# Counting samples by plain comparisons, summed on TensorE and ScalarE, and centring x right behind X W0, in a four-layer graph kernel

## The chip, the cores and the metric

The kernel runs on one core of a Trainium2 chip. A core has five engines that run side by side, each with a queue of its own that it works through in order: TensorE (PE, with its weight loads as PEld), VectorE (DVE), ScalarE (ACT), GpSimd (POOL) and SyncE (SP), which here only issues transfers. They wait for each other by semaphores. The metric is the device time of one execution in microseconds; the median over several runs counts.

## The reference

The input is `x` (2708 x 128), a weighted adjacency `adj` (2708 x 2708, non-negative and sparse, but stored dense), and the weights of four layers. Each layer is `x = layernorm(x + layer(x, adj))`. The two layers that matter here are 0 and 1:

```python
# layer 0
A_hat = A + eye;  degree = A_hat.sum(axis=1);  d = degree ** -0.5
h = (d[:, None] * A_hat * d[None, :]) @ X
return h @ W.T + b
# layer 1
XW = X @ W
Z1 = leaky_relu(s_row[:, None] + s_col[None, :], 0.01)   # s_row, s_col: XW times two vectors
den = exp(Z1);  num = A @ den
att = where(num != 0, den / num, 0)
return A @ (att @ XW)
```

Layer 2 is a hyperbolic graph convolution, layer 3 a sum over signed neighbours; both multiply by the whole adjacency once or more. They lie behind the change and are not touched by it.

## The kernel before

Features are kept as rows: `x` lies in memory as 128 feature partitions by 2708 nodes. Nodes are cut into 22 tiles of 128 (`NT`) and into 6 column blocks of up to 512 (`NB`). The kernel passes through four stages.

*Stage 1, loads and degrees.* L837 computes z = X W0 per node tile (`node_major_products`), evicted by ScalarE. Then for each column block c the adjacency tiles A(d, c), d = 0..5, are loaded by SyncE (`load_tile`, one MB each), VectorE adds them into `part` (L1084, L1086), `degrees(c, part)` (L870) folds `part` further and multiplies it by ones on TensorE (`deg`, L880), ScalarE takes the root (L891), and VectorE scales rows of z. `multiply` (L855, the products at L860) adds z times A into one PSUM accumulator per block. After blocks 0 and 1, `centred` (L921) subtracts the feature mean from three blocks of x each: a TensorE product with `centre_w`, copied back into x by ScalarE. ScalarE also checks every tile for negative entries (L1060).

*Stage 2, the end of layer 0 and the head of layer 1.* A loop over c = 0..4 (L1111) has three parts per turn. Each part issues a third of the last products of block c (`last_products`). In between, for block c-1, come `norm_roots` (variance on TensorE, root on ScalarE, reciprocal and split into three terms on VectorE), `normed` (spreading by TensorE, `rs`, and multiplication into x by VectorE), `projected` (x times W1 and the two attention vectors on TensorE, `xw`, copied out by ScalarE into `rc` and `xw`), `clamped`, and for block c-2 or c-1 `count`. Blocks 4 and 5 are finished behind the loop (L1129 to L1143).

*Counting.* The nodes are to be sorted by their attention scores into 26 groups (`GM`) of at most 126. For this, 384 scores are taken as `samples` (the scores of tiles 1 to 3), and for each of the 22 tiles and each of two scores the kernel asks of every sample how many nodes lie above it, and of every node how many samples it lies below. `count` does both in a single VectorE instruction per tile and score, 44 in all (L1041): `counts = (samples > node) + counts`, with the row sum going to `counted`.

*Stage 3, sorting.* L1176 to L1181 sum `counts` over the partitions on TensorE (`below`), VectorE derives limits (`lim`, `jp`, `prev`) and follows the group borders in a chain of 26 steps (`jk`, L1228); then come each node's group, slot and the lists. Meanwhile TensorE computes `whole_sum` (L790, products at L797), a product of exponentials `e1` with the whole adjacency, four steps at first (L1161) and the others spread over the sorting. `e1` comes from ScalarE (L1159).

*Stage 4* is the grouped attention and layers 2 and 3, from 240 us to the end.

The order in stages 2 and 3 is written by hand: under `with queued(E)` every instruction on engine E is issued behind the last one that was queued on E. So for TensorE, ScalarE and VectorE the order of the queue is the order of the calls in the program. Outside of `queued`, a scheduler orders the instructions.

PSUM has eight banks: `acc0` to `acc5` and a pair `ps` which is used in turn.

Of the kernel before, what the change touches and what calls it, by code (L numbers as in the profile page):

```python
# [21 lines left out]
P = 128  # L22
# [35 lines left out]
def kernel(  # L58
# [655 lines left out]
    counts = col.tile([P, 2, NS], BF16, tag="counts", name="counts")  # L714
    nc.gpsimd.memset(counts, 0.0)
    counted = col.tile([P, 2, NT + 1], F32, tag="counted", name="counted")
    nc.gpsimd.memset(counted[:, :, 0:1], 0.0)
# [72 lines left out]
    def whole_sum(n):  # L790
        if not tot:
            tot.extend(acc_tile(i, f"t1_{i}") for i in range(2))
# [42 lines left out]
    with tc.tile_pool(name="tri", bufs=1) as tp:  # L835
        z = q_b.rearrange("p (t f) -> p t f", f=F)
        node_major_products(w0T_s, F, lambda t0, m, ps: nc.scalar.copy(z[:, t0 : t0 + m, :], ps))  # L837
        dcol = c_tile("dcol")
# [31 lines left out]
        def degrees(c, part):  # L870
# [7 lines left out]
            for i, t in enumerate(ts):  # L878
                kw = rows(t)
                nc.tensor.matmul(  # L880
                    pd[:kw, i : i + 1], lhsT=part[:, 0, i * P : i * P + kw], rhs=ones[:, 0:1], start=True, stop=True
                )
# [37 lines left out]

        def centred(blocks):  # L921

            for b in blocks:
                w, cs = width(b), bslice(b)
                xc = ps_tile(f"xc{b}")
                nc.tensor.matmul(xc[:, :w], lhsT=centre_w, rhs=x[:, cs], start=True, stop=True)
                nc.scalar.copy(x[:, cs], xc[:, :w])
# [107 lines left out]

        def count(c, a=0, b=8):


            with queued(DVE):
                for t, i in itertools.islice(itertools.product(tiles(c), range(2)), a, b):  # L1040
                    nc.vector.scalar_tensor_tensor(  # L1041
                        counts[:, i, :],
                        samples,
                        cmp_v[:, i, t : t + 1],
                        counts[:, i, :],
                        op0=ALU.is_gt,
                        op1=ALU.add,
                        accum_out=counted[:, i, t + 1 : t + 2],
                    )

# [18 lines left out]
        for c in range(NB):  # L1069
# [3 lines left out]
            for d in range(NB):  # L1073
# [11 lines left out]
                elif d > 1:  # L1085
                    nc.vector.tensor_add(part[:, :nt, :w], part[:, :nt, :w], at[d][:, :nt, :w])  # L1086
# [4 lines left out]
            scaled, rooted[:] = degrees(c, part)  # L1091
            for d in range(NB - 2, NB):
                check(d, c, at[d])
            if c < 2:
                centred(range(3 * c, 3 * c + 3))
# [15 lines left out]
        for c in range(NB - 1):  # L1111
            for part in range(3):
                last_products(c, part)
                if c and part == 0:
                    norm_roots(c - 1)
                    if c > 1:
                        count(c - 2, 4, 7)
                elif c and part == 1:
                    normed(c - 1)
                    if c > 1:  # L1120
                        count(c - 2, 7)
# [9 lines left out]
        count(NB - 3, 1, 3)  # L1131
        norm_roots(NB - 2)
        norm_roots(NB - 1)
        count(NB - 3, 3, 6)
        normed(NB - 2)
        normed(NB - 1)
        count(NB - 3, 6)
        projected(NB - 2)
        projected(NB - 1)
        clamped(NB - 2)  # L1140
        count(NB - 2)
        clamped(NB - 1)
        count(NB - 1)  # L1143

# [4 lines left out]
    with ctx_keep:  # L1149
# [16 lines left out]
        with tc.tile_pool(name="sort", bufs=1) as st_p:  # L1166
# [7 lines left out]
            below_s = [acc_tile(4 + i, f"below{i}") for i in range(2)]  # L1174
            with queued(PE):
                nc.tensor.matmul(below_s[0][:, :NS], lhsT=ones_b, rhs=counts[:, 0, :], start=True, stop=True)  # L1176
            for i in range(2):
                if i:
                    nc.tensor.matmul(below_s[i][:, :NS], lhsT=ones_b, rhs=counts[:, i, :], start=True, stop=True)
# [728 lines left out]
```

## Time and profile before

| | us |
|---|---|
| median of 3 runs | 934.11 (933.47 to 936.2) |
| the profiled execution | 931.1 |
| its span | 929.4 |
| PE busy in the span | 856.4 (92%) |
| DVE busy | 564.3 (61%) |
| ACT busy | 369.6 (40%) |
| POOL busy | 152.5 (16%) |

A profile line of a group of instructions names the line of the kernel, the engine, the operation, what it writes and reads, the shapes and the count. In a timeline the first two numbers are start and length in us; a bracket behind gives the idle time before the instruction and what ended it. In the chain of waits, the program is followed back from its last instruction to whatever released each step. A row of stretches gives for each engine its busy time and number of instructions in that stretch, then the granted TensorE clock (1.00 is full), the share in which the DMA engines were busy, and GB/s.

The stages stand in the trace as follows: stage 1 from 0 to about 118 us, stage 2 to about 182 us, stage 3 to about 240 us, stage 4 to 929.4 us. The 44 counts run from 135.5 to 182.0 us.

### The profile page before, as it was taken

What the parts mean: (1) busy time and instruction counts of PE and PEld (TensorE: products, weight loads), DVE (VectorE), ACT (ScalarE), POOL (GpSimd) and SP (SyncE); (2) the same over time, 40 slices, a digit from 0 to 9 for tenths busy, and PEclk for the clock granted to TensorE, in tenths of its full rate; (3) what the DMA queues carried; (4) which work ended last, traced back from release to release, by engine and by line L of the source; (5) the groups of instructions that cost most, each with busy time, mean ns of one, the idle gap of its engine ahead of it and who ended that gap; (6) DMA issues with size and microseconds to landing.
All of it is one profiled execution on the core that took longest, in us unless ns stands there. A gap on an engine that the chain in (4) does not pass through costs nothing.

```text
span 929.4 us, 9409 instructions
## 1 busy us (share of the span) xinstructions
PE 856.4 (92%) x3268; PEld 428.0 (46%) x3268; DVE 564.3 (61%) x1221; ACT 369.6 (40%) x601; POOL 152.5 (16%) x182
## 2 busy tenths in 40 slices
PE   3799988579799999999999999989999999999997
PEld 2344534235344444444444444454344455555555
DVE  4895569898488888878786222637554464333222
ACT  3885332110677777566664111536332221000000
POOL 5321000303655554222110000000000000000000
PEclk9799999798799999999999999999999999999999
DMA  9997492195596555344431876477956293746410
GB/s 338 373 351 240 52 310 67 43 386 217 172 356 204 163 154 162 121 131 138 150 120 44 290 268 240 152 253 258 334 186 226 63 343 115 250 144 242 142 55 15
DMA packets 95834, 182.84 MB, mean 197 GB/s; under 512 B 6430, under 2 KB 23535, under 8 KB 95652
## 3 DMA queue, kind: packets, MB, share of 16 engines
q1 hardware_dynamic: 85556, 142.37, 44.5%
q0 software_dynamic: 8352, 37.76, 12.9%
q10 hardware_dynamic: 1872, 2.04, 0.6%
q8 instruction: 27, 0.44, 0.2%
q14 instruction: 27, 0.22, 0.1%
HBM read 179.33 MB, written 2.84 MB: 196 GB/s over the span
## 4 chain that ended last, share of the span: by engine, by line
PE 77%; DVE 14%; DMA 5%; ACT 2%; issue 2%; ACTq 0%; DVEq 0%
PE a L1518 21%; PE uacc L1426 14%; PE a L1797 11%; PE a L860 9%; PE num L1461 7%; PE a L1806 6%; DVE att L1474 4%; DMA A<-in_adjT_dram 4%; PE t L797 2%; DVE jk L1228 2%; DVE att L1455 2%; DMA cb<-in_adjT_dram 1%; PE pp L1755 1%; DVE counts L1041 1%; PE low L1293 1%
## 5 line engine op out<-in xcount | busy, mean ns | idle before, releaser
L1426 PE MATMUL uacc<-att,xw_g 128*128 128x512 f32 (+1 forms) x312 | 130.4, 554 | 8.9 <-DVE att L1474 8.2
L1466 ACT ACTIVATE ln<-num,inval,occ_l 128x512 f32<-128x512 f32 (+1 forms) x156 | 106.5, 722 | 65.7 <-DVE gat L1465 63.3
L1797 PE MATMUL a<-cb,ut 128*128 128x512 f32 (+2 forms) x264 | 124.8, 554 | 0.4 <-DMA cb<-in_adjT_dram 0.4
L1806 PE MATMUL a<-mask,node 128*128 128x512 f32 (+2 forms) x264 | 119.5, 534 | 0.0
L1461 PE MATMUL num<-gat,w_all 128*128 128x512 f32 (+1 forms) x276 | 114.1, 543 | 0.0
L1518 PE MATMUL a<-cb,q_b 128*128 128x512 f32 (+2 forms) x264 | 110.3, 555 | 1.7 <-DMA cb<-in_adjT_dram 1.7
L1518 PE MATMUL a<-cb,xw 128*128 128x512 f32 (+2 forms) x264 | 107.4, 550 | 0.0
L860 PE MATMUL a<-A,q_b 128*128 128x512 f32 (+2 forms) x264 | 105.8, 549 | 0.0
L1417 POOL DMA_INDIRECT gat<-in_adjT_dram,row_i x52 | 78.4, 1508 | 146.4 <-PE num L1461 79.4
L1426 PEld LDWEIGHTS uacc<-att,xw_g 128*128 128x128 f32 x312 | 55.8, 189 | 90.7 <-issue 50.0
L1465 DVE COPY gat<-num 2x512 f32<-2x512 f32 x150 | 86.0, 608 | 3.3 <-PE num L1461 3.1
L1474 DVE TENSOR_TENSOR att<-att,ln 128x1354 f32<-128x1354 f32 x52 | 81.1, 1560 | 9.6 <-ACT ln L1473 9.6
L1455 DVE TENSOR_SCALAR att<-q_b,gj_l 128x1354 f32<-128x1354 f32 x52 | 47.8, 921 | 37.8 <-PE uacc L1426 37.8
L1806 PEld LDWEIGHTS a<-mask,node 128*128 128x128 f32 (+1 forms) x264 | 47.7, 190 | 49.3 <-issue 47.5
L1461 PEld LDWEIGHTS num<-gat,w_all 128*128 128x128 f32 x276 | 51.2, 191 | 41.4 <-issue 22.7
L1473 ACT ACTIVATE ln<-ln 128x1354 f32<-128x1354 f32 x52 | 69.3, 1333 | 1.3
L1785 DVE TENSOR_SCALAR mask<-cb 128x3072 fp32r<-128x3072 f32 (+5 forms) x24 | 33.5, 1394 | 58.8 <-PE a L1806 58.6
L860 PEld LDWEIGHTS a<-A,q_b 128*128 128x128 f32 (+1 forms) x264 | 45.6, 190 | 47.9 <-issue 46.9
L1518 PEld LDWEIGHTS a<-cb,xw 128*128 128x128 f32 (+1 forms) x264 | 45.0, 190 | 46.3 <-issue 46.3
L1518 PEld LDWEIGHTS a<-cb,q_b 128*128 128x128 f32 (+1 forms) x264 | 44.6, 189 | 46.2 <-issue 42.3
L231 ACT ACTIVATE sq_l<-s 128x512 f32<-128x512 f32 (+1 forms) x11 | 6.6, 604 | 147.1 <-DVE s L1815 116.7
L1060 ACT ACTIVATE xw<-A 128x2048 f32<-128x2048 f32 (+3 forms) x36 | 57.0, 1583 | 8.2 <-issue 4.4
(446 smaller groups left out, 904.7 us busy)
## 6 DMA issues: line engine op xcount, KB each, us to landing
cb<-in_adjT_dram SPq DMA_DIRECT2D x15, 2816.0 KB
cb<-in_adjT_dram SPq DMA_DIRECT2D x15, 2560.0 KB
A<-in_adjT_dram SPq DMA_DIRECT2D x25, 1024.0 KB
B<-in_adjT_dram SPq DMA_DIRECT2D x18, 1024.0 KB
cb<-in_adjT_dram SPq DMA_DIRECT2D x3, 814.0 KB
cb<-in_adjT_dram SPq DMA_DIRECT2D x3, 740.0 KB
ut<-in_adjT_dram SPq DMA_DIRECT2D x2, 1024.0 KB
A<-in_adjT_dram SPq DMA_DIRECT2D x5, 296.0 KB
```

Of the source, the lines that this page charges most:

```text
L860: nc.tensor.matmul(acc[c][:, :w], lhsT=z[:kw, k, :], rhs=t[:kw, i, :w], start=c not in begun, stop=(d == NB - 1 and k == NT - 1), skip_gro ...
L1417: return nc.gpsimd.indirect_dma_start(out=gat[g], out_offset=None, in_=adj_h, in_offset=bass.IndirectOffsetOnAxis(ap=row_i[:, h, g : g + 1 ...
L1426: nc.tensor.matmul(uacc[c][:, : cb - ca], lhsT=xw_g[:, g, :], rhs=att[:, ca:cb], start=(g == 0), stop=(g == GM - 1),)
L1455: nc.vector.tensor_scalar(att, q_b[:, h0 : h0 + HALF], gj_l[:, g : g + 1], 1.0, op0=ALU.mult, op1=ALU.max)
L1461: nc.tensor.matmul(num[:, : cb - ca], lhsT=(w_first if g < FIRST else w_all)[:, g, :], rhs=gat[g][:, ca:cb], start=True, stop=True)
L1465: nc.vector.tensor_copy(gat[g + 1][0:2, ca:cb], num[0:2, : cb - ca])
L1466: nc.scalar.activation(ln_n[:, ca:cb], num[:, : cb - ca], AF.Ln, scale=occ_l[:, g : g + 1], bias=inval[:, g : g + 1],)
L1473: nc.scalar.activation(ln_n, ln_n, AF.Exp, scale=-1.0)
L1474: nc.vector.tensor_mul(att, att, ln_n)
L1518: nc.tensor.matmul(acc[:, :w], lhsT=weights[:kw, k, :], rhs=pc[:kw, t, :w], start=(k == 0), stop=(k == NT - 1),)
L1797: nc.tensor.matmul(acc[:, :w], lhsT=edge[:ke, k, :], rhs=pc[:ke, t, :w], start=(k == 0), stop=False, skip_group_check=True,)
L1806: nc.tensor.matmul(acc[:, :w], lhsT=node[:kw, k, j, :], rhs=mask[:kw, t - ma, :w], start=False, stop=(k == NT - 1 and j == 1), skip_group_ ...
```

## The change

It has four parts.

1. `count` becomes a plain comparison: `above = samples > node`, bf16, in a buffer of its own (five in rotation). A new `count_up` sums what is pending: TensorE multiplies `above` by ones into one of four groups of 32 rows of a PSUM tile (`acc0`), by the parity of the tile and the score, and ScalarE reads `above` with a Relu whose accumulator gives the row sum for `counted`. It is called in every part of the loop and between the last steps behind it.
2. The sum over partitions behind it reads the four row groups, copied once out of PSUM, with selecting weights `kind`; `lim` is one instruction; the test for the group uses the count itself with the opposite sign, so `upto` goes.
3. `centred` goes; all six blocks are centred right behind X W0.
4. In column block 0 the last tile A(5, 0) is not added by VectorE; `degrees` adds its two filled row tiles on TensorE.

PSUM banks of `whole_sum` and of the slots (`low`) move by one, since `acc0` is taken longer.

```diff
-    counts = col.tile([P, 2, NS], BF16, tag="counts", name="counts")
-    nc.gpsimd.memset(counts, 0.0)
-    counted = col.tile([P, 2, NT + 1], F32, tag="counted", name="counted")
+    counted = col.tile([P, 2, NT], F32, tag="counted", name="counted")
+    kind = const.tile([P, 2], F32, tag="kind", name="kind")
...
         node_major_products(w0T_s, F, lambda t0, m, ps: nc.scalar.copy(z[:, t0 : t0 + m, :], ps))
+
+        for b in range(NB):
+            w, cs = width(b), bslice(b)
+            xc = ps_tile(f"xc{b}")
+            nc.tensor.matmul(xc[:, :w], lhsT=centre_w, rhs=x[:, cs], start=True, stop=True)
+            nc.scalar.copy(x[:, cs], xc[:, :w])
...
+                terms = [] if more is None else [more[:, q, :] for q in range(2)]
+                terms.append(part[:, 0, :])
+                for q, a in enumerate(terms):
+                    nc.tensor.matmul(
+                        pd[:kw, i : i + 1],
+                        lhsT=a[:, i * P : i * P + kw],
+                        rhs=ones[:, 0:1],
+                        start=(q == 0),
+                        stop=(q == len(terms) - 1),
+                    )
...
         def count(c, a=0, b=8):
-            with queued(DVE):
-                for t, i in itertools.islice(itertools.product(tiles(c), range(2)), a, b):
-                    nc.vector.scalar_tensor_tensor(
-                        counts[:, i, :], samples, cmp_v[:, i, t : t + 1], counts[:, i, :],
-                        op0=ALU.is_gt, op1=ALU.add, accum_out=counted[:, i, t + 1 : t + 2])
+            for t, i in itertools.islice(itertools.product(tiles(c), range(2)), a, b):
+                above = tp.tile([P, NS], BF16, tag="above", name=f"above{t}_{i}", bufs=5)
+                with queued(DVE):
+                    nc.vector.tensor_scalar(above, samples, cmp_v[:, i, t : t + 1], None, op0=ALU.is_gt)
+                pending.append((t, i, above))
+
+        def count_up():
...
+            for t, i, above in pending:
+                j = 2 * (t % 2) + i
+                with queued(PE):
+                    nc.tensor.matmul(
+                        counts_of["below"][32 * j : 32 * j + 32, :NS],
+                        lhsT=ones_b[:, :32],
+                        rhs=above,
+                        start=(t < 2),
+                        stop=(t >= NT - 2),
+                        skip_group_check=True,
+                    )
+                with queued(ACT):
+                    nc.scalar.activation(counts_of["junk"], above, AF.Relu, accum_out=counted[:, i, t : t + 1])
+            pending.clear()
...
-                elif d > 1:
+                elif d > 1 and (d, c) != (NB - 1, 0):
...
-            scaled, rooted[:] = degrees(c, part)
+            scaled, rooted[:] = degrees(c, part, at[NB - 1] if c == 0 else None)
...
-            if c < 2:
-                centred(range(3 * c, 3 * c + 3))
...
-                if c and part == 0:
-                    norm_roots(c - 1)
-                    if c > 1:
-                        count(c - 2, 4, 7)
-                elif c and part == 1:
-                    normed(c - 1)
-                    if c > 1:
-                        count(c - 2, 7)
+                if c and part < 2:
+                    (normed if part else norm_roots)(c - 1)
+                if pending:
+                    count_up()
+                if c > 1 and part < 2:
+                    count(c - 2, *((7, 8) if part else (4, 7)))
...
         summed_up(NB - 1)
-        count(NB - 3, 1, 3)
         norm_roots(NB - 2)
+        count_up()
         norm_roots(NB - 1)
-        count(NB - 3, 3, 6)
+        count(NB - 3, 1, 4)
         normed(NB - 2)
+        count(NB - 3, 4, 6)
+        count_up()
         normed(NB - 1)
+        projected(NB - 2)
         count(NB - 3, 6)
-        projected(NB - 2)
+        count_up()
         projected(NB - 1)
         clamped(NB - 2)
-        count(NB - 2)
+        count(NB - 2, 0, 4)
+        count_up()
         clamped(NB - 1)
+        count(NB - 2, 4)
+        count_up()
         count(NB - 1)
+        count_up()
...
+            counts = srt([P, NS], "counts", F32R)
+            nc.vector.tensor_copy(counts, counts_of["below"][:, :NS])
```

## The prediction

> **What bounds the kernel now.** I read the page, then the busy time by stretches, then the chain of waits over the stretch that the change edits, then single instructions there. Only 0 to 190 us are edited; from 190 us on, sorting, attention and products are the same instructions and start from one result, the `below` matmuls of L1176. So the question is when `below` is done (184.3 us), and whether what follows moves with it. It does: behind it come the VectorE chain `jp`, `prev`, `jk` and the slots, without a wait that an outside event sets.
>
> Busy time by stretches (length, then PE, PEld, DVE, ACT, POOL, clock, DMA):
>
> ```profile
> 140.00:149.00 9.00, 8.00 (x40) 3.75 (x41) 8.79 (x28) 2.35 (x7) 0.00 (x0) 1.00 0.37 118
> 149.00:159.00 10.00, 9.14 (x49) 4.81 (x47) 9.12 (x30) 2.36 (x7) 0.19 (x1) 1.00 0.09 26
> 159.00:168.00 9.00, 5.65 (x38) 3.21 (x36) 8.57 (x26) 2.64 (x9) 0.00 (x0) 0.95 0.10 32
> ```
>
> VectorE looks like the bound (8.79 of 9.00), but TensorE is as full in the first two rows: two engines are near their limit, and relief of one meets the other. ScalarE has room.
>
> The chain of waits in order of time (start, length, what):
>
> ```profile
> 172.00 2.98 PE xw L993 x12
> 175.01 0.16 ACT rc L1002
> 175.17 0.28 ACT xw L1003
> 175.47 1.28 ACT L1159
> 176.76 0.21 ACT e L1159
> 176.97 0.04 issue
> 177.02 6.72 PE t L797 x58
> 183.74 0.27 PE below L1176
> ```
>
> This matters most. ScalarE's exponential (L1159, with its table load) releases TensorE's `whole_sum(4)` (6.72 us), and `below` is queued behind that. The last 12 counts run on VectorE at 174.76 to 182.05 beside it, and end 1.6 us before TensorE is free: they are hidden.
>
> Single instructions (start, length, engine):
>
> ```profile
> 145.97 0.37 ACT L972 ACTIVATE work<-var,eps_c 128x128 f32<-128x128 f32 x1 [0.94 <-PE var L252]
> 146.51 0.95 DVE L974 RECIPROCAL work<-work 128x128 f32<-128x128 f32 x1
> 148.81 0.40 PE L273 MATMUL rs<-work,sel 128*128 128x128 bf16 x4 [1.00 <-DVE work L267]
> 155.74 0.37 ACT L972 ACTIVATE work<-var,eps_c 128x128 f32<-128x128 f32 x1 [1.83 <-PE var L252]
> 156.14 0.95 DVE L974 RECIPROCAL work<-work 128x128 f32<-128x128 f32 x1 [0.67 <-ACT work L972]
> 158.44 0.40 PE L273 MATMUL rs<-work,sel 128*128 128x128 bf16 x4 [0.86 <-DVE work L267]
> 118.58 0.44 ACT L1060 ACTIVATE xw<-A 128x296 f32<-128x296 f32 x1
> 118.93 0.18 ACT L1060 ACTIVATION_READ_ACCUMULATOR xw<-A 128x1 f32 x1
> ```
>
> In the first loop counting delays the reciprocal by 0.14 us after the root; in the second VectorE itself waits 0.67 us. TensorE waits 1.00 and 0.86 us for `rs` in these loops: that is all VectorE can give them.
>
> **What the Trainium skill says.** "VectorE: DVE Perf Modes", section Mode 2×_2P: a single-source fp32 operation with both ends in SBUF does two elements per cycle. The trace agrees: `att` of L1455, 1354 elements, takes 0.92 us, below one per cycle (1.41). "ScalarE: Activation LUTs", section What ACT_TABLE_LOAD costs: an ACTIVATE with immediates takes 186 ns + 0.833 ns an element, overlapping by about 93 ns; the 296-element row above (0.44, accumulator read after 0.35) fits. Same page, Table sets: relu is in every set, so no load is added; L1060 and L891 run here after one load. "TensorE: Matmul & The Clock Gate", Part 3: matmuls of 32 output columns run beside each other; the eight `var` matmuls (0.43 us together) agree.
>
> **The change part by part.**
>
> *Comparisons.* Before, 44 fused compare-and-add run 0.54 us apart. Now they are plain comparisons: 384/1.92 = 0.20 us plus a fixed 0.14 (0.54 less 384/0.96; `ohs`, 128 elements, runs 0.163 apart): 0.34. Bounds: 0.26 if only synchronization remains, 0.54 if the double rate fails. VectorE sheds 44 x 0.20 = 8.8 us.
>
> *Sums on TensorE.* 44 matmuls of 384 bf16 columns. L1176 and L1179 give 0.17 us each alone; in column groups four may cost as little as 0.2 together. They stand in TensorE's queue. The four after `norm_roots` fit into the wait for `rs`. The next three stand between `rs` and the last products, and wait for three comparisons that VectorE starts only after the split into terms: 3 x 0.34 + 0.06 + 0.17 - 0.05 = 1.20 us after the start of `rs` instead of 0.23, so 0.97 lost; one more before `xw` costs 0.17. So 1.14 for each of the loops c = 2, 3, 4. Against that the reciprocal comes 0.25 earlier in c = 2, about 0.1 in c = 3, and 0.48 in the first count (139.94 to 139.46). Sum: 3 x 1.14 - 0.83 = +2.6. Bounds: -1.7 (the three TensorE waits shrink and the matmuls cost little) to +4.5.
>
> *After the loop.* Two comparisons fewer before the reciprocals and three cheaper ones give some 1.5 us; `rs` of block 5 now stands behind five sums, and `rc` of block 5 behind seven ScalarE sums: the same again and a little more. I take +0.3.
>
> *Sums on ScalarE.* Each is 384 elements: 0.35 + 88 x 0.00078 = 0.42, and 0.10 to the next after the accumulator read: 0.52 back to back, 0.64 if the accumulator read is waited for (the rows of 104.86 us stand 0.82 apart at 592 elements). In the loops ScalarE is 26% busy and takes them, behind each root in its queue. But the last 12 belong to blocks 4 and 5, follow the last `xw` copy, and the exponential of L1159 is issued behind them. So table load, exponential, `whole_sum(4)` and `below` all move by 12 x 0.55 = 6.6 us (6.2 to 7.7). What hid the counts, `whole_sum(4)`, is now behind them.
>
> *Centring.* Six blocks of two matmuls leave 29.4 to 34.9 and 45.2 to 48.6 us and go behind X W0, where TensorE stands idle for 9.28 us before 27.71; ScalarE's six copies (3.3 us) fall into its idle 4.42 us there. Up to 61 us the loads fill the DMA queues (DMA share 1.05, 375 GB/s) and VectorE's partial sums keep pace with 0.2 to 0.4 us to spare, so the first stretch gives nothing. Of the second, 1.82 + 0.52 = 2.3 us are in TensorE's chain, which is unbroken to 117 us. But the degree matmul of 60.46 waits for VectorE until 60.22 anyway; the gain exists only as far as products with A(0,3), which lands at about 59, are put ahead of it. Bounds 0 to 2.3; I take 1.3.
>
> *Degrees of column 0.* One addition of 1.3 us leaves VectorE and eight matmuls come (some 1.0 to 1.8 us by the two `deg` rows, 1.02 and 1.84 for eight instructions). Under the DMA bound: 0, with +1 if it overruns the 0.2 us to spare.
>
> *The rest.* The copy of `counts` (about 0.56 as `samples` L1032) lies beside `whole_sum`; `upto` (0.20) and a `lim` (0.16) leave; bank numbers change: 0. DMA reloads of `B` start later by the same shift as their readers, so nothing more.
>
> Sum: 2.6 + 0.3 + 6.6 - 1.3 = +8.2 us. The profiled execution took 931.1 us (span 929.4 and 1.7 around it): 939.3. It lies 3.0 below the median of 934.11, so on the median I forecast 942.3, rounded 942.
>
> **The rivals.**
> 1. *The loops are VectorE's alone.* For it: 8.79 of 9.00. Against: TensorE's waits there sum to about 3 us, and VectorE waited 0.67. If 32 comparisons before `rc` of block 5 save 0.28 each, `rc` comes 9.0 earlier; -9.0 + 6.6 - 1.3 = -3.7: 930.4, faster. It decides from 8.1 us won before the last `xw` copy.
> 2. *Centring wins nothing*, since column 2's degrees are set by loads (or the scheduler puts the matmuls elsewhere): +9.5, 943.6.
> 3. *The dear ends*: comparisons at one per cycle (3 loops x 3 x 0.2 = 1.8), ScalarE sums at 0.64 (1.1): +11.1, 945.2.
> 4. *The cheap ends*: -1.7 in the loops, 6.2 in the tail, -2.3 for centring, nothing after the loop: +2.2, 936.3, inside what measurement tells from no change.
>
> **How the numbers follow.** About 0.3% (2.8 us) is what can be told from no change. Chances: my forecast 0.45, rival 2 0.22, rival 3 0.13, rival 4 0.10, rival 1 0.10. Slower 0.80, same 0.10, faster 0.10. The forecast's own range is 938 to 945; with half of rival 4 and rival 3 it becomes 937 to 946.
>
> **What would show it.** Right: ScalarE runs 12 Relu with accumulators between the last `xw` copy and the exponential, over 6 us; `whole_sum` starts that much later against `rc` of block 5; distances between `rs` of 9.7 to 10.8 instead of 8.87 and 9.63; no `xc` after 27 us. Wrong: `rc` of block 5 before 170 us, an exponential ahead of the sums, or ScalarE sums shorter than 0.4 us. A first stage longer than before would show that the early `xc` delays the degrees of column 0.

## The result, and the profile after

The change makes the kernel slower: 947.71 us median (946.71 to 949.74, 4 runs) against 933.79 (933.06 to 936.2, 4 runs), a ratio of 1.0147 with a 95% interval of 1.0122 to 1.0172. The same kernel, run again later beside others, gave 950.63 (947.12 to 950.97, 5 runs), ratio 1.0183 (1.0161 to 1.0204). The forecast was 942, from 937 to 946.

Both kernels were profiled twice in the end, so that a difference can be told from the spread of one kernel. In us from the start of the span; `rs` is the first spread of a block, distances run from start to start, and the last two rows lie behind the change:

| | before, two profiles | after, two profiles | forecast of the change | measured |
|---|---|---|---|---|
| degree sums of block 1 start | 44.34, 45.26 | 46.05, 46.15 | | |
| first `rs` (end of stage 1) | 130.09, 131.10 | 131.23, 131.33 | -1.3 | +0.7 |
| first `rs` to that of block 4 | 37.59, 38.79 | 41.93, 40.69 | +2.6 | +3.1 |
| that to the last copy of `xw` | 7.39, 7.40 | 8.77, 8.78 | +0.3 | +1.4 |
| that to `below` | 8.60, 6.73 | 16.09, 16.29 | +6.6 | +8.5 |
| `below` to the first `num` | 60.10, 60.00 | 60.06, 59.75 | 0 | -0.1 |
| `num` to the end of the span | 685.6, 685.6 | 687.6, 688.6 | 0 | +2.5 |

"Measured" is the difference of the two means. From the second row on the rows sum to 16.1, which is the difference between the profiled times (947.42 and 947.12 against 931.1 and 931.35). A mean of two is worth about a microsecond here: the columns show how far one kernel differs from itself.

First what the engines do in the loops. Busy time by stretches of the kernel after, in the columns of before (length, then PE, PEld, DVE, ACT, POOL, clock, DMA):

```profile
140.00:149.00 9.00, 8.56 (x40) 3.69 (x42) 6.90 (x19) 6.41 (x22) 0.00 (x0) 1.00 0.19 57
149.00:159.00 10.00, 9.30 (x51) 4.74 (x44) 7.26 (x19) 7.17 (x23) 0.34 (x1) 1.00 0.10 27
159.00:168.00 9.00, 8.30 (x42) 3.44 (x40) 5.52 (x13) 5.87 (x21) 0.00 (x0) 1.00 0.01 3
```

VectorE has fallen from 8.79 to 6.90 us in the first row: it was relieved as intended. ScalarE has risen from 2.35 to 6.41. TensorE, full before, is full still, and the loops are longer. What one comparison and its two sums cost, for all 44 (shortest, median and longest in ns, then first and last start):

```profile
L1053 DVE TENSOR_SCALAR above<-samples,cmp_v x44: 401/414/2366, 137.8 to 187.7; 128x384 bf16<-128x384 f32 x44
L1065 PE MATMUL counts<-above,ones_b x44: 322/326/502, 139.0 to 188.2; 128*32 128x384 bf16 x44
L1074 ACT ACTIVATE above_j<-above x44: 511/523/536, 139.5 to 189.3; 128x384 bf16<-128x384 bf16 x44
L1074 ACT ACTIVATION_READ_ACCUMULATOR above_j<-above x44: 185/186/203, 139.9 to 189.8; 128x1 f32 x44
```

The comparison is cheap: 0.41 us long, three of them in 1.07 us, 0.33 apart where the forecast took 0.34. One of the 44 is not; it lasts until a GpSimd instruction beside it has ended:

```profile
184.27 2.67 POOL L1177 MEMSET xw<- 2x2816 f32 x1 [30.29 <-DMA xw_d<-xw]
184.80 2.37 DVE L1053 TENSOR_SCALAR above<-samples,cmp_v 128x384 bf16<-128x384 f32 x1 [0.23 <-ACT above_j L1074]
```

The sum on ScalarE is not cheap either: 0.52 us and 0.19 for reading out its accumulator.

One turn of the loop, single instructions of the kernel after in order of start (start, length, engine, line):

```profile
160.65 0.95 DVE L983 RECIPROCAL work<-work 128x128 f32<-128x128 f32 x1 [1.82 <-ACT work L981]
...
162.81 1.07 DVE L1053 TENSOR_SCALAR above<-samples,cmp_v 128x384 bf16<-128x384 f32 x3
...
162.95 0.40 PE L273 MATMUL rs<-work,sel 128*128 128x128 bf16 x4 [0.69 <-DVE work L267]
...
163.28 0.98 PE L1065 MATMUL counts<-above,ones_b 128*32 128x384 bf16 x3
...
164.19 2.18 PE L870 MATMUL a<-A,q_b 128*128 128x512 f32 x4
```

VectorE now waits 1.82 us for the root, where it had counted before. TensorE still waits 0.69 us ahead of `rs`, and then its last products stand behind three sums: they start 1.24 us after `rs`, where they started 0.23 after it.

The chain of waits at the end of the stretch:

```profile
189.32 0.61 ACT above_j L1074 x2
189.96 1.28 ACT L1189
191.25 0.21 ACT e L1189
...
191.51 6.58 PE t L801 x58
198.09 0.37 PE below L1210
```

The same exponential and the same `whole_sum` as in the first profile of before, 14.5 us later. What is ahead of them on ScalarE, right behind the last copy of `xw` (181.93 to 182.30):

```profile
182.20 0.53 ACT L1074 ACTIVATE above_j<-above 128x384 bf16<-128x384 bf16 x1
182.62 0.20 ACT L1074 ACTIVATION_READ_ACCUMULATOR above_j<-above 128x1 f32 x1
182.85 0.52 ACT L1074 ACTIVATE above_j<-above 128x384 bf16<-128x384 bf16 x1
...
189.96 1.28 ACT L1189 ACT_TABLE_LOAD   x1
```

Twelve sums, 0.645 us apart, from 182.20 to 189.94: 7.7 us, and the table load starts when the last one is done.

### The profile page after: what moved, and what is told of

Its sections match the earlier page's. It is cut to its first block, busy times and chain, and to the rows that moved or that the text cites. A ratio compares the mean times of both kernels' runs of the same rounds, so it can differ in the third digit from the quotient of the medians.

```text
span 945.7 us, 9626 instructions
## 1 busy us (share of the span) xinstructions
PE 874.5 (92%) x3328; PEld 435.8 (46%) x3328; DVE 557.5 (59%) x1175; ACT 396.2 (42%) x689; POOL 151.2 (16%) x186
## 4 chain that ended last, share of the span: by engine, by line
PE 75%; DVE 15%; DMA 2%; issue 2%; ACT 2%; ACTq 0%; DVEq 0%
PE a L1554 21%; PE uacc L1462 13%; PE a L1833 11%; PE a L870 9%; PE num L1497 7%; PE a L1842 6%; DVE att L1510 5%; DMA cb<-in_adjT_dram 2%; DVE att L1491 2%; DVE jk L1266 2%; PE t L801 1%; PE pp L1791 1%; DVE ut L1112 1%; PE xw L1002 1%; DVE work L983 1%
## 5 line engine op out<-in xcount | busy, mean ns | idle before, releaser
L870 PE MATMUL a<-A,q_b 128*128 128x512 f32 (+2 forms) x264 | 110.3, 568 | 2.3 <-DVE q_b L912 2.2
```

What stands on the lines that cost most here:

```text
L870: nc.tensor.matmul(acc[c][:, :w], lhsT=z[:kw, k, :], rhs=t[:kw, i, :w], start=c not in begun, stop=(d == NB - 1 and k == NT - 1), skip_gro ...
```

## The experiments

All times are medians; a ratio is to runs of the kernel before on the same chip.

| run | time | ratio, 95% interval |
|---|---|---|
| exp_first | 940.22 | 1.0059 (1.0042 to 1.0075) |
| later_three | 944.72 | 1.0119 (1.0100 to 1.0138) |
| comb (both) | 938.15 | 1.0042 (1.0024 to 1.0061) |
| comb2 | 935.94 | 1.0020 (1.0009 to 1.0031) |
| comb3 | 936.16 | 1.0019 (1.0006 to 1.0033) |
| loop_end | 947.31 | 1.0159 (1.0131 to 1.0188) |
| xc_back | 952.68 | 1.0182 (1.0156 to 1.0208) |
| more_back | 948.98 | 1.0158 (1.0140 to 1.0177) |
| both_back | 951.02 | 1.0171 (1.0143 to 1.0200) |
| filler | 947.11 | 1.0131 (1.0104 to 1.0158) |
| after_again | 950.63 | 1.0183 (1.0161 to 1.0204) |
| both_again | 948.60 | 1.0170 (1.0145 to 1.0195) |
| before_xc | 933.84 | 0.9990 (0.9971 to 1.0009) |
| before_early | 932.27 | 0.9986 (0.9976 to 0.9996) |
| before_two | 931.32 | 0.9972 (0.9959 to 0.9985) |

The medians are of 4 or 5 runs, of 12 to 22 for comb, comb2, comb3 and the last three. A sixteenth run, before_again, is the kernel before for its second profile (931.35, one execution).

Differences between two rows are often no larger than their intervals: those of after (1.0122 to 1.0172) and later_three overlap, those of exp_first and comb, of comb and comb2, of comb2 and comb3 too. Where that is so, the distances in the profiles carry the argument.

### The tail: the exponential ahead of the last twelve sums

In exp_first the exponential and `whole_sum(4)` go ahead of the sums of blocks 4 and 5; the twelve comparisons get room in `q_b`, so that none waits for a buffer.

```diff
         projected(NB - 1)
+        with queued(ACT):
+            nc.scalar.activation(e1[:, : tiles(1)[0]], rcl[:, 0, : tiles(1)[0]], AF.Exp)
+        with queued(PE):
+            whole_sum(4)
         clamped(NB - 2)
```

> The changed kernel with the exponential of the first four columns and the first four steps of the whole sum issued right behind the last projection, ahead of the last 12 comparisons' sums; the 12 comparisons get places of their own in a tile that is free by then, so that VectorE does not wait for ScalarE. Theory (the 12 row sums on ScalarE, 0.645 us each, stand between the last projection and the exponential, and the whole sum waits for it): the exponential starts about 1.5 us behind the last copy instead of 9, the below products end about 5 us earlier (near 193 instead of 198.9 us), time near 942.5 us. Rival (the counts themselves, by VectorE's pace and TensorE's sums, set the below products anyway): a gain under 1 us.

The time fell by 7.5 us against after (947.71 to 940.22), more than the 5 that the theory gave: this is the largest part of the loss. From the `rs` of block 4 to `below` it is 19.1 us instead of 24.9 and 25.1, so 5.9 of it can be placed. In the profile of exp_first, by single instructions:

```profile
184.34 0.38 ACT L1012 COPY xw<-xw 128x256 f32<-128x256 f32 x1
...
184.73 1.28 ACT L1171 ACT_TABLE_LOAD   x1
...
186.29 6.74 PE L801 MATMUL t<-B,e 128*1 128x512 f32 x71 [2.05 <-ACT e L1171]
...
192.99 0.65 PE L1069 MATMUL counts<-q_b,ones_b 128*32 128x384 bf16 x9
...
193.94 0.56 DVE L1210 CAST counts<-counts 128x384 fp32r<-128x384 f32 x1 [3.81 <-ACT above_j L1078]
```

The table load follows the last copy at once, as before the change, and from there to `below` (194.56) it is 10.2 us instead of 16.1. It is still more than the 6.7 and 8.6 us of before. TensorE's last nine sums (0.65 us) and the copy of the counts out of PSUM (0.56) now stand behind `whole_sum`. And the last line shows a wait: TensorE's sums end at 193.64, but the copy starts only at 193.94, behind ScalarE's last sum (its read-out ends at 193.86), although it reads only what TensorE has written. That is 0.3 us here; it grows when `whole_sum` goes ahead.

Two later runs follow that up. comb2 is comb (exp_first and later_three, below, together) with the exponential right behind the last root and the four steps of `whole_sum` spread over TensorE's waits:

```diff
         norm_roots(NB - 1)
+        with queued(ACT):
+            nc.scalar.activation(e1[:, : tiles(1)[0]], rcl[:, 0, : tiles(1)[0]], AF.Exp)
         count(NB - 3, 1, 4)
         normed(NB - 2)
+        with queued(PE):
+            whole_sum(1)
...
         projected(NB - 1)
-        with queued(ACT):
-            nc.scalar.activation(e1[:, : tiles(1)[0]], rcl[:, 0, : tiles(1)[0]], AF.Exp)
         with queued(PE):
-            whole_sum(4)
+            whole_sum(3)
```

comb3 is comb2 with the copy and the limits put elsewhere:

```diff
-            counts = srt([P, NS], "counts", F32R)
+            counts = q_b[:, 6 * NS : 7 * NS]
...
-                        lhsT=kind_r[:, i : i + 1].to_broadcast([P, P]),
+                        lhsT=kind[:, i : i + 1].to_broadcast([P, P]),
```

> After with both repairs: the exponential and whole_sum(4) ahead of the last 12 sums, and the three sums of each loop behind its last products. Theory (two separate losses): the gains add, 947.7 - 7.5 - 3.0 = 937.2. Rival (both shorten the same stretch): 940, no better than the first alone.

> As the run with both repairs, and the exponential moves to right behind the last root, so that no table load stands behind the last copies of xw; one step of whole_sum goes behind the spread of block 4, three behind the projection of block 5. Theory (the tail waits for ScalarE's table load and for whole_sum's four steps): the sum below some 3 us earlier than in the run with both repairs, 933 to 935. Rival (below then waits for the last comparisons and sums of block 5): 936 to 937.

> The third repair with the copy of the counts and the limits placed in memory that ScalarE's last sums do not use (a free part of q_b); the two below products then run in full fp32, some 0.9 us dearer together. Theory (the copy waited for ScalarE because its tile lies where the buffers of those sums lie): the copy starts right behind TensorE's last sum, about 2.8 us earlier against the spread of block 4 than in the run before with the late copy; lim some 2 us earlier, the time 933 to 935. Rival (the copy waits for TensorE's sums or the bank, and the release named is a coincidence): it starts where it did, and the time is 936 to 937.

comb came out at 938.15, nearer to the sum of the two repairs (937.2) than to no addition (940): 9.6 us off 947.71, against 7.5 and 3.0 alone. comb2 lies another 2.2 lower. In its profile TensorE's last sum is done at 185.7, and the copy stands idle until ScalarE is:

```profile
188.55 0.56 DVE L1212 CAST counts<-counts 128x384 fp32r<-128x384 f32 x1 [4.55 <-ACT above_j L1078]
```

In comb3 the same copy goes right behind TensorE:

```profile
186.24 0.56 DVE L1212 COPY q_b<-counts 128x384 f32<-128x384 f32 x1 [0.41 <-PE counts L1069]
```

Against the `rs` of block 4 it starts 15.10 us later instead of 16.98, 1.9 us earlier where the theory had 2.8. So the wait was for memory, not for data: the tile of the copy belongs to the sorting, whose memory is taken over from the buffers of stage 2, and ScalarE's last sums still write one of these (`above_j`). The time did not fall. One comparison again lasted 2.68 us beside GpSimd's memset, and TensorE's last two sums waited 1.58 us for it, which comb2 was spared. And the two `below` products in full fp32 cost 1.6 us each where they had cost 0.4 to 0.7: `lim` comes 18.5 us after the `rs` of block 4 instead of 18.9. That the place of the tile made the copy wait is shown, a gain from moving it is not. No version with the changed counts became faster than the kernel before.

### The loops: three sums behind the last products instead of ahead of them

```diff
-                if pending:
+                if pending and part != 1:
                     count_up()
```

> The changed kernel with the three sums that stand between the spread (rs) and the last products moved behind those products, in the loop's three turns with counts. Theory (TensorE, in order, waits there for three comparisons): the distances between spreads of 10.05 and 10.95 us shrink by 0.6 to 0.9 us each, in all 1.8 to 2.7 us, time near 945.4 us. Rival (the turns are set by the latency from variance to spread or by the clock): distances shrink by less than 0.2 us each and the time stays at 947.7 us.

The median is 3.0 us below that of after; the theory had 1.8 to 2.7. The same turn of the loop, TensorE in later_three:

```profile
158.96 0.40 PE L273 MATMUL rs<-work,sel 128*128 128x128 bf16 x4 [0.70 <-DVE work L267]
159.19 2.13 PE L870 MATMUL a<-A,q_b 128*128 128x512 f32 x4
161.25 0.35 PE L1065 MATMUL counts<-above,ones_b 128*32 128x384 bf16 x4
```

The products start 0.23 us after `rs` again, and all four sums, now without a wait for VectorE, take 0.28 us together up to the next matmul, where three had taken 0.91. The distances between the `rs` of blocks 1 to 4 are 9.01, 9.91 and 9.17 us, against 10.05, 10.95 and 10.21 in after and 8.87, 9.63 and 9.24 in before: 0.35 us of the 3.5 that the three loops lost are left.

### Behind the loop: the projection of block 4 behind five sums

In the kernel after, TensorE and VectorE behind the loop:

```profile
176.14 0.67 DVE L993 TENSOR_TENSOR x<-work,rs 128x512 f32<-128x512 f32 x1
...
176.73 0.73 DVE L1053 TENSOR_SCALAR above<-samples,cmp_v 128x384 bf16<-128x384 f32 x2
...
177.19 0.81 PE L1065 MATMUL counts<-above,ones_b 128*32 128x384 bf16 x2 [0.45 <-DVE above L1053]
...
177.93 0.39 PE L273 MATMUL rs<-work,sel 64*128 64x128 bf16 x2
...
178.25 2.10 PE L1002 MATMUL xw<-w1ext,x 128*128 128x130 f32 x8
```

x of block 4 is ready at 176.8, but its projection is queued behind two sums whose comparisons VectorE makes after that multiplication. loop_end holds TensorE's seven sums of block 3 back until the projection of block 5 (`count_up(True)` issues ScalarE's sums alone) and leaves ScalarE's where they are; the seven comparisons are kept in `q_b`:

```diff
         count(NB - 3, 4, 6)
-        count_up()
+        count_up(True)
...
         count(NB - 3, 6)
-        count_up()
+        count_up(True)
         projected(NB - 1)
```

> After with the TensorE sums of block 3's last seven comparisons moved behind the projection of block 5 (their comparisons and ScalarE's sums stay where they are). Theory (the projection of block 4 stands in TensorE's queue behind five sums, two of which wait for comparisons that end at 177.5, while its x is ready at 176.8): from the spread rs of block 4 to the last copy of xw 7.4 us instead of 8.8, the time 1.0 to 1.4 us below after. Rival (ScalarE's seven sums ahead of the copies hold them back, or VectorE does): 8.5 to 8.8, no gain.

From the `rs` of block 4 (171.20) to the last copy of `xw` (178.66) it is 7.46 us: what the change had added there is gone, and TensorE in loop_end shows it:

```profile
173.32 0.39 PE L273 MATMUL rs<-work,sel 64*128 64x128 bf16 x2 [1.72 <-DVE work L267]
174.90 2.97 PE L1002 MATMUL xw<-w1ext,x 128*128 128x130 f32 x12 [1.19 <-DVE x L993]
177.79 0.83 PE L1071 MATMUL counts<-q_b,ones_b 128*32 128x384 bf16 x7
```

Seven sums in one go take 0.83 us. Of the gain of 1.3, some 0.7 us reach `below` (24.2 us behind the `rs` of block 4, against 24.9 and 25.1). That is too small for the medians: 947.31 against 950.63 in the same set of runs and 947.71 in the first, with intervals that overlap.

### Stage 1: the early centring and the degrees of column 0

xc_back puts the centring back behind blocks 0 and 1, more_back adds A(5, 0) on VectorE again, both_back and both_again do both, so that only the changed counts are left.

```diff
-        for b in range(NB):
...
-            nc.scalar.copy(x[:, cs], xc[:, :w])
...
+            if c < 2:
+                centred(range(3 * c, 3 * c + 3))
```

```diff
-                elif d > 1 and (d, c) != (NB - 1, 0):
+                elif d > 1:
...
-            scaled, rooted[:] = degrees(c, part, at[NB - 1] if c == 0 else None)
+            scaled, rooted[:] = degrees(c, part)
```

> The changed kernel with the centring of x put back behind the degrees of blocks 0 and 1, all else as changed. Theory A (the six early copies on ScalarE, and the PSUM pair that they hold, keep the first degrees and their root waiting): the first root comes at 30 to 30.8 us instead of 31.34, the first spread of block 0 (rs, 131.23 us in the changed kernel) comes 0.5 to 1.2 us earlier, and the time falls by about 1 us from 947.7. Theory B (the eight more degree matmuls are what delays the first root): no change within 0.3 us at the root; and the 2.3 us of centring are back in TensorE's chain after 45 us, so the time may even rise by up to 2 us.

> The changed kernel with the degrees of column 0 as before (VectorE adds the last tile, four degree products), centring still early. Theory A (ScalarE's early copies hold up the root): the root stays at 31 to 31.4 us, no change of time beyond 0.5 us. Theory B (the extra degree matmuls): the root comes at 30 us or sooner and rs of block 0 about 1.1 us earlier, time about 946.5 us.

> After with parts 3 and 4 undone together: x is centred behind blocks 0 and 1 as before, A(5,0) is added by VectorE; the changed counts stay. Theory (the two parts together cost stage 1 about a us, each alone is worse since it makes another gap): first spread rs at about 130.1 as before, median 945.5 to 946.5. Rival (the two parts are a gain that the counts eat): rs as late as with either part alone, 132 to 135, median 949 to 952.

> After with parts 3 and 4 undone, again, with more executions. If the two parts are a real gain beside the changed counts: 3 us above the run before it (950 to 952). If the first result came from where the clock fell: within 1.5 us of it.

> The kernel after, unchanged, as the partner of the next run: 947 to 948.5. In this second profile the stretch from the first to the second spread rs is 9.5 us if the clock stays full there, 10.7 if it falls as in the first profile.

The medians mislead here. The first three (952.68, 948.98, 951.02) all lie above after, as if both parts were gains; the repetition reversed the pair (both_again 948.60, after_again 950.63). Neither part can be seen in the time. The first `rs` misleads too: in xc_back and more_back it came at 134.93 and 132.52 us, later than in after, against both theories, and in both_back and both_again at 131.53 and 133.73.

What moves it is the clock between the degree sums of blocks 1 and 2. From 45 to 54 us, xc_back and then both_back (columns as above):

```profile
45.00:54.00 9.00, 7.89 (x18) 4.46 (x19) 6.96 (x10) 4.85 (x9) 0.08 (x1) 0.62 1.06 379
45.00:54.00 9.00, 8.30 (x26) 4.21 (x27) 7.36 (x9) 7.25 (x11) 0.00 (x0) 1.00 1.06 382
```

At half rate for 6.8 us, that distance is 19.2 us in xc_back; without a fall it is 16.1 in both_back. With the early centring it is 16.4 where the clock falls for 3.4 us (after and seven others) and 18.1 to 18.5 where it falls for longer (more_back, exp_first, comb2). The kernel before is not spared: its stage 1 took 16.1 us there in two profiles and 17.5 in before_early. The six profiles with 17.5 us or more are the six with the latest first `rs` (132.5 to 134.9; all others 130.1 to 132.0), whatever parts they contain.

The landmarks, starts of single instructions in the trace, can tell more, since some distances in stage 1 repeat to 0.02 us. The first root starts at 28.9 to 30.0 us in the eight profiles with the old degrees of column 0 and at 29.7 to 32.1 in the ten with the new ones, on average 29.6 and 31.0: theory B, that the eight matmuls delay it, fits better than theory A. The degree sums of blocks 3 and 4 lie 21.49 to 21.52 us apart in every kernel with the old centring (before, before_again, before_early, xc_back, both_back, both_again) and 20.63 to 20.64 in after, after_again, more_back, before_xc and before_two. Between them TensorE multiplies without a break: 48 products in before, 46 in before_xc. Between the degree sums of blocks 1 and 2 it is the other way round, 30 and 32. So the early centring lets exactly two products be done earlier, 2 x 0.43 us. Against that the degree sums of block 1 start at 45.95 on average over nine profiles with the new degrees of column 0 (45.35 to 46.83; all but filler) and at 45.24 over the eight with the old ones (44.34 to 45.67): the new degrees cost about what the centring gains. And from the degree sums of block 1 to those of block 2 it is 16.4 us instead of 16.1, although six centring matmuls have left that stretch, since the clock falls there. Nothing is left, and a kernel before with the early centring alone shows no gain either:

> The kernel before with part 3 alone: x is centred right behind X W0. My prediction gave this 1.3 us (0 to 2.3), so 933.4; the pairs of runs with and without it (951.0 against 949.0, 952.7 against 947.7) say 2 to 5, so 930 to 932.5. If the gain there came only from the place of the gaps in those kernels, 934.7 or more.

0.999, with 1 inside its interval. The interval excludes more than 2.7 us, so most of the two to five that the first pairs had suggested; the 1.3 of the forecast it neither shows nor excludes.

filler tests another suspicion. In after TensorE stands idle for 2.14 us ahead of the degree sums of block 1, its clock is at half rate for a while behind that, and the products up to block 2 take longer. filler keeps TensorE busy there:

```diff
+            if c == 1:
+                for _ in range(3):
+                    nc.tensor.matmul(pd[:, P:], lhsT=ident, rhs=part[:, 3, : BW - P], start=True, stop=True)
```

> After with three extra products of 384 columns in TensorE's idle time ahead of the degree sums of block 1, written into unused columns and read by nobody. Theory (TensorE's clock falls because it stands idle for 2.1 us there, and the slow clock then stretches the 32 products up to the degree sums of block 2): clock 1.00 instead of 0.81 in 45 to 54 us, the degree sums of block 2 and the first spread rs one to two us earlier than in after, median about 946. Rival (the clock follows something else, or block 2 is set by VectorE and the loads): no landmark earlier, 947.7 within a us.

The clock did stay at 1.00, and the 32 products took 14.0 us instead of 15.7. From filler:

```profile
47.61 13.98 PE L870 MATMUL a<-A,q_b 128*128 128x512 f32 x32
62.36 0.80 PE L896 MATMUL deg<-ones,ut 128*128 128x1 f32 x6 [0.77 <-DVE ut L885]
```

From after:

```profile
46.94 15.68 PE L870 MATMUL a<-A,q_b 128*128 128x512 f32 x32
```

But the degree sums of block 2 start at 62.36, against 62.45 in after. filler delays itself: its degree sums of block 1 start at 46.70 instead of 46.05. From these to those of block 2 it is 15.7 us instead of 16.4, and the last 0.77 are a wait for VectorE's additions. So a fall of 3.4 us costs after some 0.7 us there, not the one to two that I expected, and filler spent this on its own products. The time did not change (947.11). What the clock costs in stage 1 is large only where the fall is longer, as in the six profiles above.

> The kernel before, unchanged, for a second profile of it. If its first profile (931.1, some three below the median of its runs) was a lucky execution, stage 1 is longer in this one: the first spread rs at 131 to 132.5 instead of 130.09, and the time 933 to 936. If stage 1 repeats within 0.3 us, rs stands at 130.1 and the later stage 1 of the kernels after is their own.

before_again shows that stage 1 does not repeat within 0.3 us: it ends 1.0 us later, nearly as late as in after, and in the first loop the clock fell (below). Its time, 931.35, is no nearer to the median than that of the first, which the expectation had at 933 to 936.

### The kernel before with an earlier exponential

The tail suggests a change to the kernel before: the exponential needs only scores that are known long before, so it can go behind the last root, where ScalarE and TensorE stand idle, and the steps of `whole_sum` into TensorE's waits.

```diff
         norm_roots(NB - 1)
+        with queued(ACT):
+            nc.scalar.activation(e1[:, : tiles(1)[0]], rcl[:, 0, : tiles(1)[0]], AF.Exp)
         count(NB - 3, 3, 6)
         normed(NB - 2)
+        with queued(PE):
+            whole_sum(1)
         normed(NB - 1)
+        with queued(PE):
+            whole_sum(1)
...
         projected(NB - 1)
+        with queued(PE):
+            whole_sum(2)
```

> The kernel before with the exponential right behind the last root and the four steps of whole_sum put into TensorE's waits (one behind the spread of block 4, one behind that of block 5, two behind the projection of block 5). Theory (the end of the stage is the chain of copy, table load, exponential and whole_sum; counts are done 1.6 us before it): the sum below then waits for the counts, 182.1 instead of 183.7 in the profile, the time 1 to 2 us lower, 932.7 to 933.7. Rival (the steps of whole_sum push back the spread and projection by more than they free): no gain, 934.7 or more.

> The kernel before with both: part 3 and the early exponential. If the two are separate gains they add: 2 to 4.5 us below before, 930 to 932.7. If not, no better than the better one of them.

before_early is 0.14% faster (0.9986, 0.9976 to 0.9996), before_two, with the early centring beside it, 0.28% (0.9972, 0.9959 to 0.9985). The two intervals overlap, so that the centring adds to it is not shown. before_two has the lowest time of the study, below both kernels. The chain of waits of before_two:

```profile
171.02 1.76 PE t L797 x15
172.78 0.66 PE xw L991 x4
173.62 0.27 ACT xw L1001
174.10 0.21 DVE rcl L1009
174.68 4.31 DVE counts L1039 x16
```

Neither the table load nor the exponential is in it any more; VectorE's counts are, up to 181.85, and `below` starts at 181.44 instead of 183.67. From the `rs` of block 4 that is 13.8 us, in before_early 13.1, against 16.0 and 14.1 in the two profiles of before. The counts were hidden before by 1.6 us in one profile and by nothing in the other; now they bound the stretch.

## Why the prediction was wrong in size

The direction was right, and so was the largest mechanism: twelve sums on ScalarE ahead of the exponential. The forecast also named the loops and the stretch behind them. The sum was 5.7 us short of the first comparison of medians (8.2 against 13.9) and 7.9 short in the profiles (16.1). The steps that failed are sizes: the distance of the sums on ScalarE (0.55 us taken, 0.645 measured), the stretch behind the loop (+0.3, measured +1.4), the gain from centring (-1.3, stage 1 measured +0.7), and two terms put at nothing, the overrun of the degrees and a loss from `num` on (+2.5 in the profiles, cause open). Five terms were off, all to the same side.

- *Sums on ScalarE, "all move by 12 x 0.55 = 6.6 us (6.2 to 7.7)".* Right in mechanism, the size at the end of its range: 0.645 us apart. The forecast took 0.52 back to back and "0.64 if the accumulator read is waited for", and chose near the first; here the accumulator is read between two sums every time. The rows it had in hand gave the right figure: the checks of `A` stand 0.82 apart at 592 elements, which is 0.35 to the read-out, 0.25 for 296 more elements, and 0.22 from there to the next; with 88 more elements instead that is about 0.645. The step failed by taking 0.10 for the last term: after shows 0.42 to the read-out, as computed, and 0.23 from there to the next. By the Trainium skill, "ScalarE: Activation LUTs", What ACT_TABLE_LOAD costs, an estimate for the activation alone is 186 + 0.833 x 384 = 506 ns, and the trace agrees (523); the read-out behind it, 186 ns, and where the next may start are not in that figure. Twelve times 0.095 is 1.1 us. The rest of the measured +8.5 is the other side of the difference: in the second profile of before `whole_sum` took 4.85 us instead of 6.72, at a clock of 1.00 instead of 0.73; between the two first profiles, both with a slow `whole_sum`, the stretch is 7.5 us longer, near the 7.7 of the twelve sums.
- *After the loop, "the same again and a little more. I take +0.3".* This step failed: it is +1.4. The prediction saw that `rs` of block 5 would stand behind five sums, but not that the projection of block 4 stands behind the same five, and that two of their comparisons come after the multiplication that the projection waits for. loop_end removes it.
- *Sums on TensorE, "1.14 for each of the loops", less 0.83.* The piece itself held: the last products start 1.24 us after `rs` (1.20 computed), and the three loops are 1.19, 1.31 and 0.97 us longer. What should come back by earlier reciprocals, 0.25 and 0.1 in two of these loops, is not seen in them, and the first loop gives 0.37 back instead of 0.48 (9.48 in the second profile of after, 9.85 in the first of before, both at full clock). In all +3.1 instead of +2.6; later_three gives 3.0 of it back.
- *Centring, "I take 1.3", and degrees, 0 "with +1 if it overruns the 0.2 us to spare".* The condition that I set, only as far as products with A(0, 3) are put ahead, was the right one: two products were, 0.87 us. The degrees overran, by some 0.7 on average over all profiles, though the ranges touch. And the clock, which the forecast left out, falls where the centring had kept TensorE busy. Together nothing is left, where I took -1.3.
- *"Sorting, attention and products are the same instructions" from 190 us on.* From `below` to `num` that held to 0.3 us. Behind it the profiles of the kernel after show 2.5 us more. Two waits of TensorE for loads of `cb` are longer (3.2 us instead of 1.7 and 1.8 for L1518, 0.9 to 1.0 instead of 0.3 to 0.4 for L1797), but a wait of 2.3 us ahead of `pr` for VectorE goes in return, and in sum TensorE's idle time is no longer (17.6 and 16.1 us against 17.3). What is longer is the busy time of the same matmuls, 665.5 and 667.9 us instead of 663.8: behind the longer wait the clock falls to half rate for 3.4 us in both profiles of after (from 638.8 and 637.8) and in neither of before. The other profiles with the changed counts show 2.0 us or more as well, but before_early and before_two also show 1.3. Why the loads of `cb` come later is open, and also whether the loss is in the medians: comb2's profiled time lies 3.3 us above its median, while both profiled times of before lie some 3 below theirs, which I can't explain.

What was priced right: the comparison (0.34 forecast, 0.33), the place of the exponential, and that the relief of VectorE would meet a full TensorE, so that rival 1 (930.4) fell: VectorE sheds its time and waits 1.82 us for the root. Rival 3, the dear ends, was the closest with 945.2; it named the ScalarE sums of 0.64 and was right in that half, but its other half, comparisons at one element per cycle, did not happen, so that it came so near is luck. Rival 2, that centring wins nothing, is right in effect; its reason, that the loads set the degrees of column 2, is not: in after TensorE reaches them without a wait.

The range failed because the terms were given their likely values and the range was put around the sum, as if their errors were independent. They were not: three of them, the sums on both engines and those behind the loop, were instructions put into a queue ahead of something, and each time I counted the instruction and only part of what stood behind it.

## What to carry to other kernels

When work is moved from a busy engine to one with room, ask for each moved instruction what stands behind it in its new queue, and give it the place behind the critical one: the same sums cost 3.5 us ahead of the last products and 0.35 behind them, and twelve sums cost 6 to 7.5 us only because an exponential that did not need them stood behind. Price an accumulating activation with its read-out, as the distance between two starts in a run of them. And profile the unchanged kernel twice before reading a difference of a microsecond.

## What the runs showed of the hardware

*The clock falls behind the same wait in some executions and not in others.* Ahead of the first `rs` TensorE waits 1.62 to 1.63 us in both kernels. From 131 to 140 us the second profile of before (columns as above):

```profile
131.00:140.00 9.00, 8.90 (x38) 5.40 (x39) 5.51 (x19) 2.36 (x7) 0.00 (x0) 0.81 1.05 378
```

and the second of after:

```profile
131.00:140.00 9.00, 8.45 (x43) 4.11 (x43) 6.20 (x17) 3.83 (x12) 0.00 (x0) 1.00 1.06 378
```

In the first profiles it was the other way round, 1.00 in before and 0.81 in after. Where it falls it is at 0.50 from about 133.5 to 136.9 us, in both_back and comb to about 140.2 and in comb3 from 132.3 to 139.1, so for 3.4 or 6.8 us, and the loop from the first to the second `rs` takes 1.2 or 2.9 us longer (9.48, 10.72 and 12.38). The Trainium skill, "TensorE: Matmul & The Clock Gate", Part 1, describes a free-running window of about 3.4 us that decides on half or full rate; the lengths agree, and so does that it differs from run to run. That a whole idle window is needed, as its table has it, does not fit: TensorE was busy for 4 of the 6 us from 126 to 132 us in after, and its longest wait there was 1.63. Such a fall alone makes two profiles of one kernel differ by 1 to 3 us, here and in stage 1, so a difference of that size between two single profiles shows nothing before the clock has been compared.

*The plain comparison and a GpSimd memset hold each other up.* In twelve of the thirteen profiles with the changed counts one comparison meets the memset of `xw` and takes 2.4 to 2.8 us instead of 0.41; it ends 0.2 us behind the memset each time. In comb2 the comparisons end undisturbed and the memset takes 3.05 us instead of 2.44. The fused instruction of before ran beside the same memset in 0.61 us, its usual length.

*Sums in column groups are as cheap as hoped only when nothing is waited for.* Four of 384 columns into four row groups start within 0.01 us of each other in later_three, and the next matmul 0.28 us behind them; behind three comparisons that arrive 0.33 us apart, each takes its own 0.33.

*A wait for memory looks like a wait for data.* The copy of the counts was released by an engine whose result it does not read; giving it another place moved its releaser from ScalarE to TensorE.
